# Two PSUM banks instead of three per leaf pair, the imaginary sum added by TensorE, and two block sums moved in the last batch

## The chip, the cores and the metric

The kernel runs on one core of a Trainium2 chip. The metric is the device time of one execution in microseconds; three runs are shown, and the profile comes from one further execution. The engines are named as in the profile: PE is TensorE (PEld its weight loads), DVE is VectorE, ACT is ScalarE, POOL is GpSimd, SP is SyncE, which here only issues DMAs.

## The reference

Two graph layers over 64 graphs of 256 nodes with 256 features each, all in float32. What matters here is the first layer's convolution branch:

```python
xc = jnp.transpose(x, (0, 2, 1))
h = relu(bn1(conv1d(xc, conv1_w)))            # kernel size 1
h = bn2(conv1d(h, conv2_w, pad=8))            # 17 taps, 256 -> 256 channels
x_conv = jnp.transpose(relu(h + xc), (0, 2, 1))
A = exp(-dist(x @ w_se.T)) * adj              # message passing
x_nmp = A @ relu(x @ w_msg.T + b_msg)
gi = concat([x_conv, x_nmp]) @ w_ih.T + b_ih  # a GRU cell: r, z and n parts
gh = x @ w_hh.T + b_hh
nn_ = tanh(gi_n + r * gh_n)
x1 = layernorm(x + (1 - z) * nn_ + z * x)
```

The second layer normalises x1, multiplies by the adjacency and by two weights, adds, applies relu, adds x1 and normalises again.

## The kernel before

The 64 graphs are worked in 8 batches of 8. Each batch has a convolution, `conv(b)`, which is a Python generator that emits a few instructions at a time, and each graph has a per-graph part (gates, message passing, update, second layer). While batch b's eight graphs are emitted, `pump()` (line 1180) takes steps from `conv(b + 1)` in between. The order of the instructions on every engine is the order of emission; nothing reorders it later[...]. The convolution of batch b+1 is therefore interleaved with the graphs of batch b at fixed places, the same in each of the batches 1 to 7. Batch 0's convolution runs alone at the start, and the graphs of batch 7 run alone at the end (lines 1246 to 1278).

The 17-tap convolution is done by transforms. DVE splits the signal by butterflies into leaves (`split_all`, `split_u`, lines 342 to 374); each leaf is a complex number per channel, held as a real slot `re` and an imaginary slot `im` in the SBUF tile XF, and `sums` slots hold re + im. A complex product takes three real products with the transformed weights: k1 = sums·w0, k2 = re·w1, k3 = im·w2, and then re' = k1 − k3 and im' = k1 + k2. Leaves are taken in pairs: `products(b, first, sums)` (line 389) emits the matmuls of one pair and returns a function `take` that is called later, after some butterflies, and brings the results to SBUF. There are seven such pairs per batch, numbered 0 to 6 below, and then `last_products` (line 429). Each real product gives 128 rows by 256 channels and is two matmuls of 128x256 (`product`, line 383), and every float32 matmul leaves two records in the trace, so a pair has 24 records.

The weights w0, w1, w2 of one leaf come by one DMA of 768 KB from DRAM into a buffer of a pool of three (`load_w`, line 376, `bufs=3`; the issue is line 380 on SP's queue). Loads take the three buffers in turn; a load's issue waits on SP's queue until the buffer's last reader, a matmul, is done, and everything behind it on SP waits too. In batch 0 the weights are all in SBUF already.

PSUM has eight banks, handed out in turn by `bank()` (line 100), so an allocation waits for the readers of the one eight before it.

For batch 0, `products` hands over to `products_added` (line 409), which has another form: it uses two banks, emits k1's matmuls (records 0 to 7 of the pair), has ACT copy k1 to SBUF (line 418), emits k3's (records 8 to 15), and then adds k2's matmuls onto the bank of k1 (records 16 to 23), so that TensorE forms im'. Its `take` copies im' with ACT (line 425) and forms re' with DVE (line 426). For batches 1 to 7 the three products go to three banks, leaf by leaf; `take` copies k1 with ACT (line 404) and forms re' and im' with DVE (lines 405 and 406).

In the last batch, `block_gates(k)` (line 814) forms the gates from block products, after `block_sums(k, i)` (line 798) has made sums of blocks of the operands on DVE, four operations for each of three operands (i = 0 for x, 1 for the passed messages, 2 for the convolution). Its fourth step is x's part of n: eight matmul records (line 856) and one DVE addition (line 858).

Of the kernel before, what the change touches and what calls it, by code (L numbers as in the profile page):

```python
# [17 lines left out]
B, N, D = 64, 256, 256  # L18
# [16 lines left out]
def leaf_angles(phi, m):  # L35

    if m == 1:
        return [phi]
    return leaf_angles(phi / 2, m // 2) + leaf_angles(phi / 2 + PI, m // 2)
# [8 lines left out]
LEAVES = [(V + k, V + 8 + k, a) for k, a in enumerate(leaf_angles(PI / 2, 8))]  # L48
# [28 lines left out]
def gnn_two_layers(  # L77
# [17 lines left out]
    nc = tc.nc  # L95
# [4 lines left out]
    def bank(name):  # L100
        return psum.tile([P, 512], F32, tag="ps", name=name)
# [143 lines left out]
    def sl(a, n, step=1):  # L245
        return X[:, a:a + n] if step == 1 else X[:, a:a + (n - 1) * step + 1:step]
# [129 lines left out]
    def load_w(b, first, n):  # L376
        if b == 0:
            return lambda m, c: W2[0][:, c, first + m, :]
        t = work.tile([P, 3, C, D], F32, tag="w2", name="w2", bufs=3)
        nc.sync.dma_start(out=t[:, :n], in_=w2m[first:first + n].rearrange("f c p o -> p f c o"))  # L380
        return lambda m, c: t[:, m, c, :]

    def product(ps, slot, w, m, first=True):

        for c in range(C):
            nc.tensor.matmul(ps, X[:, slot, c * P:(c + 1) * P], w(m, c), start=first and c == 0, stop=(c == C - 1),  # L386
                             skip_group_check=True)

    def products(b, first, sums):

        if b == 0:
            return products_added(first, sums)
        p1, p2, p3 = bank("ps_k1"), bank("ps_k2"), bank("ps_k3")
        re, im, _ = LEAVES[first]
        for k in range(2):
            w = load_w(b, 3 * (first + k), 3)
            at = slice(k * D, (k + 1) * D)
            product(p1[:, at], sums + k, w, 0)
            product(p2[:, at], re + k, w, 1)
            product(p3[:, at], im + k, w, 2)  # L400

        def take():
            k1 = sl(sums, 2).rearrange("p s e -> p (s e)")
            nc.scalar.copy(k1, p1)
            nc.vector.tensor_sub(sl(re, 2).rearrange("p s e -> p (s e)"), k1, p3)
            nc.vector.tensor_add(sl(im, 2).rearrange("p s e -> p (s e)"), k1, p2)
        return take

    def products_added(first, sums):

        p1, p3 = bank("ps_k1"), bank("ps_k3")
        re, im, _ = LEAVES[first]
        w = [load_w(0, 3 * (first + k), 3) for k in range(2)]
        at = [slice(k * D, (k + 1) * D) for k in range(2)]
        k1 = sl(sums, 2).rearrange("p s e -> p (s e)")
        for k in range(2):
            product(p1[:, at[k]], sums + k, w[k], 0, k == 0)
        nc.scalar.copy(k1, p1)
        for k in range(2):
            product(p3[:, at[k]], im + k, w[k], 2)  # L420
        for k in range(2):
            product(p1[:, at[k]], re + k, w[k], 1, False)

        def take():
            nc.scalar.copy(sl(im, 2).rearrange("p s e -> p (s e)"), p1)
            nc.vector.tensor_sub(sl(re, 2).rearrange("p s e -> p (s e)"), k1, p3)
        return take
# [222 lines left out]
    def load(k):  # L650

        if k >= B:
            return
        load_xt(k)
        load_adj(k)
# [9 lines left out]
    def load_x(k):  # L665
        if k < B:
            XG[k] = work.tile([P, C, D], F32, tag="x", name="x")
            nc.sync.dma_start(out=XG[k], in_=x[k].rearrange("(c p) d -> p c d", p=P))
# [129 lines left out]
    def block_sums(k, i):  # L798

        if i == 2:  # L800
            xc, g = XC[k]
            v = xc[:, :, g, :]
        else:
            v = (XT, NMP)[i][k]
        a11, a12, a21, a22 = (v[:, c, n * P:(n + 1) * P] for n in range(C) for c in range(C))
        at = S * D + ((k % 2) * 3 + i) * 4 * P
        s1, s2, s3, s4 = (XF[:, at + j * P:at + (j + 1) * P] for j in range(4))
        nc.vector.tensor_add(s1, a21, a22)
        nc.vector.tensor_sub(s2, s1, a11)
        nc.vector.tensor_sub(s3, a11, a21)  # L810
        nc.vector.tensor_sub(s4, a12, s2)
        LEFT[k, i] = (a11, a12, s4, a22, s1, s2, s3)
# [54 lines left out]
    def update(k):  # L867

        rz, gn = RZ[k]
        nn = work.tile([P, C, D], F32, tag="nn", name="nn", bufs=1)  # L870
        stt(nn, rz[:, :, :D], 1.0, gn[:, :, D:], op0=ALU.add, op1=ALU.mult)
        stt(nn, nn, 0.5, gn[:, :, :D])
        nc.scalar.activation(nn, nn, AF.Tanh)
        yield

        w = work.tile([P, C, D], F32, tag="w", name="w", bufs=1)
        nc.vector.tensor_sub(w, XG[k], nn)
        stt(w, rz[:, :, D:], 3.0, w, op0=ALU.add, op1=ALU.mult)
        stt(w, nn, 4.0, w)
        mv = work.tile([P, C, 2], F32, tag="mv", name="mv", bufs=4)  # L880
        for n in range(C):
            stats(mv, n, w[:, n, :])


        q = work.tile([P, 2, C], F32, tag="q", name="q", bufs=4)
        nc.gpsimd.tensor_scalar(q[:, 0, :], mv[:, :, 1], 4 * EPS, None, ALU.add)
        nc.gpsimd.tensor_scalar(q[:, 1, :], mv[:, :, 1], 1 + EPS, 4 * EPS * EPS, ALU.mult, ALU.add)
        nc.gpsimd.tensor_tensor(q, q, mhalf[:, :2 * C].rearrange("p (a c) -> p a c", a=2), ALU.pow)
        sh = work.tile([P, C], F32, tag="sh", name="sh", bufs=4)
        nc.gpsimd.tensor_mul(sh, mv[:, :, 0], q[:, 0, :])  # L890
        nc.gpsimd.tensor_scalar(sh, sh, -1.0, None, ALU.mult)  # L891
        yield
        H[k] = work.tile([P, C, D], F32, tag="h", name="h", bufs=1)
        X1[k] = work.tile([P, C, D], F32, tag="x1", name="x1", bufs=2)
        for n in range(C):
            nc.vector.tensor_scalar(H[k][:, n, :], w[:, n, :], mv[:, n, 0:1], q[:, 1, n:n + 1],
                                    ALU.subtract, ALU.mult)
        for n in range(C):
            nc.scalar.activation(X1[k][:, n, :], w[:, n, :], AF.Identity, bias=sh[:, n:n + 1], scale=q[:, 0, n:n + 1])  # L899
        yield  # L900


    def transposes_h(k):
        hT = work.tile([P, C, N], F32, tag="hT", name="hT", bufs=1)
        ps = bank("ps_hT")
        for c in range(C):
            for n in range(C):
                q = c * N + n * P
                nc.tensor.transpose(ps[:, q:q + P], H[k][:, n, c * P:(c + 1) * P], ident)
        for c in range(C):  # L910
            nc.scalar.activation(hT[:, c, :], ps[:, c * N:(c + 1) * N], AF.Identity,
                                 bias=gb[:, 1, c:c + 1], scale=gb[:, 0, c:c + 1])
        H[k] = hT

    def project(k):
        hT = H[k]
        hr = work.tile([P, C, D], F32, tag="hr", name="hr", bufs=1)
        outs = []
        for n in range(C):
            ps = bank("ps_out")  # L920
            for c in range(C):
                nc.tensor.matmul(ps, hT[:, c, n * P:(n + 1) * P], wrr[:, c, :], start=(c == 0), stop=(c == C - 1))  # L922
            nc.scalar.copy(hr[:, n, :], ps[:, :D])
            outs.append(ps)
        OUTS[k] = (hr, outs)
# [29 lines left out]
    def step(g):  # L955
        if g is not None:
            next(g, None)
# [103 lines left out]
    first = conv(0)  # L1061
# [114 lines left out]
    for b in range(NB):  # L1176
        coming = conv(b + 1) if b + 1 < NB else iter(())
        done, at, goal = 0.0, 0, BG * POINTS - 6
# [67 lines left out]
    for k in range(first_k, B - 1):  # L1246
        load(k + 3)
        load_x(k + 1)
        ga, up = block_gates(k), update(k)
        step(ga)  # L1250
        step(y_left)
        step(ga)
        transposes_h(k - 1)
        step(ga)
        passing(k + 1)
        if k + 2 < B:
            factors(k + 2)
        step(ga)
        if k + 2 < B:
            block_sums(k + 1, 0)  # L1260
            block_sums(k + 1, 2)
        project(k - 1)
        if k + 2 < B:
            distances(k + 2)
        msg = messages(k + 3) if k + 3 < B else None
        step(msg)
        step(up)
        step(msg)
        step(up)
        if k + 2 < B:  # L1270
            block_sums(k + 1, 1)
        step(up)
        if k + 2 < B:
            mask(k + 2)
        agg = aggregate(k - 1)
        step(agg)
        step(agg)
        y_left = agg
# [44 lines left out]
```

## Time and profile before

| | |
|---|---|
| median of three runs | 2246.47 us (2245.61 to 2249.44) |
| the profiled execution, its own time | 2248.85 us |
| its span (first to last instruction) | 2247.1 us |
| PE busy | 2205.1 us, 98% of the span |
| DVE busy | 1719.0 us, 76% |
| ACT busy | 773.1 us, 34% |
| POOL busy | 503.8 us, 22% |
| leaf products on PE, batches 1 to 7 (line 386) | 1316 records, 297.8 us |
| ACT copy of k1, batches 1 to 7 (line 404) | 49, 0.57 us each |
| DVE sum and difference from PSUM (lines 405, 406) | 49 each, 0.68 us each |
| load of one leaf's weights (line 380) | 105 of 768 KB, 5.8 us to landing in the median |

In the timeline a row is a stretch of equal instructions on one engine: start, length, engine, line, operation, tiles, form, count, and in brackets the engine's idle time ahead of it with what ended it. In the view of waits a row says who waited for whom: total us, times, the longest. A DMA row of SP or ACT is the issue, not the transfer.

### The profile page before, as it was taken

How to read it: one execution, taken by the hardware profiler on the slowest of the kernel's cores; microseconds unless marked ns; L12 is line 12 of the kernel's file. 1: busy time of each engine (PE TensorE's matmuls, PEld its weight loads, DVE VectorE, ACT ScalarE, POOL GpSimd, SP SyncE). 2: the span in 40 equal slices, each digit the busy share in tenths (PEclk: the TensorE clock that was granted, in tenths of full speed). 3: DMA queues.
4: the chain of work that ended last, by engine and by line, in shares of the span. 5: the costliest groups of instructions: out<-in, count | busy, mean ns of one | idle time of the engine just before them, and what ended most of it. 6: DMA issues, size and time to landing. Idle time of an engine off the chain costs nothing.

```text
span 2247.1 us, 24777 instructions
## 1 busy us (share of the span) xinstructions
PE 2205.1 (98%) x8400; PEld 1459.6 (65%) x8400; DVE 1719.0 (76%) x3322; ACT 773.1 (34%) x1594; POOL 503.8 (22%) x933
## 2 busy tenths in 40 slices
PE   8999999999999999999999999999999999999998
PEld 5776666666665676656666566666666666666665
DVE  6967988399873998649886598956989389896665
ACT  6533223532244322433224422243222532224333
POOL 0112222132122321223122231223222132122222
PEclk9999999999999999999999999999999999999999
DMA  5932442314323152233422243222432314421100
GB/s 149 318 113 66 141 135 77 103 38 151 121 76 108 54 169 83 75 103 108 139 87 76 84 131 122 76 96 69 141 116 90 99 42 137 141 71 43 43 28 20
DMA packets 212683, 226.70 MB, mean 101 GB/s; under 512 B 22103, under 2 KB 203854, under 8 KB 212558
## 3 DMA queue, kind: packets, MB, share of 16 engines
q1 hardware_dynamic: 190128, 191.27, 27.0%
q10 hardware_dynamic: 22430, 33.86, 4.3%
q8 instruction: 67, 1.10, 0.2%
q14 instruction: 58, 0.48, 0.1%
HBM read 179.22 MB, written 45.88 MB: 100 GB/s over the span
## 4 chain that ended last, share of the span: by engine, by line
PE 67%; DVE 24%; DMA 3%; issue 3%; POOL 2%; ACT 1%; SPq 0%; POOLq 0%; DVEq 0%; ACTq 0%
PE ps_k L386 14%; PE ps_rz L755 11%; DVE XF L104 9%; PE ps_rz L752 6%; PE ps_n L767 6%; PE ps_out L922 5%; PE ps_c L492 5%; PE ps_nmp L736 4%; DMA w<-w2m 3%; PE ps_msg L678 3%; PE ps_n L765 3%; PE ps_out L934 3%; DVE XF L362 2%; DVE XF L456 2%; DVE nn L104 1%
## 5 line engine op out<-in xcount | busy, mean ns | idle before, releaser
L104 DVE SCALAR_TENSOR_TENSOR XF<-XF 128x512 f32<-128x512 f32 (+2 forms) x800 | 508.0, 666 | 7.4
L386 PE MATMUL ps_k<-w,XF 128*128 128x256 f32 x1316 | 297.8, 381 | 17.6 <-DVE st L688 12.0
L386 PEld LDWEIGHTS ps_k<-w,XF 128*128 128x128 f32 x1316 | 246.7, 190 | 63.3 <-issue 24.9
L696 POOL TENSOR_TENSOR sq<-st 128x6 f32<-128x6 f32 x64 | 13.8, 215 | 1219.2 <-DVE st L688 1169.3
L922 PE MATMUL ps_out<-wrr,hT 128*128 128x512 f32 x504 | 226.7, 592 | 0.0
L759 ACT ACTIVATE rz<-rz 128x512 f32<-128x512 f32 x114 | 71.8, 630 | 446.4 <-DVE rz L758 446.4
L752 PE MATMUL ps_rz<-whh,xT 128*128 128x512 f32 x456 | 214.4, 592 | 0.0
L755 PE MATMUL ps_rz<-wih,nmp 128*128 128x512 f32 x456 | 214.3, 592 | 0.0
L755 PE MATMUL ps_rz<-wih,xc 128*128 128x512 f32 x456 | 214.3, 592 | 0.0
L768 DVE TENSOR_TENSOR gn<-ps_n,brzn 128x512 f32<-128x512 f32 x114 | 78.3, 687 | 171.2 <-PE ps_n L767 171.2
L899 ACT ACTIVATE x<-w,sh,q 128x256 f32<-128x256 f32 x126 | 68.8, 593 | 342.7 <-POOL sh L891 342.7
L755 PEld LDWEIGHTS ps_rz<-wih,xc 128*128 128x128 f32 x456 | 86.6, 190 | 109.1 <-issue 109.1
L755 PEld LDWEIGHTS ps_rz<-wih,nmp 128*128 128x128 f32 x456 | 86.6, 190 | 109.1 <-issue 109.1
L758 DVE TENSOR_TENSOR rz<-ps_rz,brzn 128x512 f32<-128x512 f32 x114 | 77.7, 682 | 104.3 <-PE ps_rz L755 104.3
L922 PEld LDWEIGHTS ps_out<-wrr,hT 128*128 128x128 f32 x504 | 95.2, 190 | 93.6 <-issue 81.8
L678 PE MATMUL ps_msg<-wms,xT 128*128 128x260 f32 x512 | 129.9, 396 | 0.0
L362 DVE TENSOR_TENSOR XF<-XF 128x512 f32<-128x512 f32 (+3 forms) x128 | 125.4, 1004 | 1.7
L736 PE MATMUL ps_nmp<-AT,msg 128*128 128x256 f32 x512 | 121.0, 379 | 0.0
L752 PEld LDWEIGHTS ps_rz<-whh,xT 128*128 128x128 f32 x456 | 82.1, 190 | 57.8 <-issue 55.0
L934 PE MATMUL ps_out<-hr,adj 128*128 128x256 f32 x504 | 119.5, 380 | 0.0
L492 PE MATMUL ps_c<-xTc,w 128*128 128x512 f32 x256 | 116.2, 596 | 2.3 <-ACT xTc L482 2.3
L765 PE MATMUL ps_n<-whh,xT 128*128 128x256 f32 x456 | 117.2, 379 | 0.0
(200 smaller groups left out, 3738.1 us busy)
## 6 DMA issues: line engine op xcount, KB each, us to landing
w<-w2m SPq DMA_DIRECT2D x105, 768.0 KB, 5.8
xn<-in_x_dram SPq DMA_DIRECT2D x32, 512.0 KB, 4.2
xt<-xTc ACTq DMA_DIRECT2D x32, 512.0 KB, 3.2
xT<-xt SPq DMA_DIRECT2D x64, 256.0 KB, 3.0
xb<-in_x_dram SPq DMA_DIRECT2D x32, 512.0 KB, 5.1
adj<-in_adjT_dram SPq DMA_DIRECT2D x64, 256.0 KB, 2.7
x<-in_x_dram SPq DMA_DIRECT2D x64, 256.0 KB, 3.0
out_dram<-y ACTq DMA_DIRECT2D x63, 256.0 KB, 2.3
```

The source lines that it names most:

```text
L104: nc.vector.scalar_tensor_tensor(o, in0, s, in1, op0=op0, op1=op1)
L362: (nc.vector.tensor_add if add else nc.vector.tensor_sub)(sl(o, n), sl(a, n), sl(b, n))
L386: nc.tensor.matmul(ps, X[:, slot, c * P:(c + 1) * P], w(m, c), start=first and c == 0, stop=(c == C - 1), skip_group_check=True)
L492: nc.tensor.matmul(pss[o], w1[:, c, o * P:(o + 1) * P], xTc[:, c, :], start=(c == 0), stop=(c == C - 1))
L678: nc.tensor.matmul(ps[:, :D + 4], XT[k][:, c, m * P:(m + 1) * P], wms[:, c, :], start=(c == 0), stop=(c == C - 1 and not idle))
L736: nc.tensor.matmul(ps[:, d * N:(d + 1) * N], MSG[k][:, m, d * P:(d + 1) * P], AT[k][:, m, :], start=(m == 0), stop=(m == C - 1))
L752: nc.tensor.matmul(prz, XT[k][:, c, q], whh[:, c, 0:2 * D], start=(c == 0), stop=False)
L755: nc.tensor.matmul(prz, ins[i], wih[:, i, 0:2 * D], start=False, stop=(j == 3))
L765: nc.tensor.matmul(pn[:, D:], XT[k][:, c, q], whh[:, c, 2 * D:], start=(c == 0), stop=(c == C - 1))
L767: nc.tensor.matmul(pn[:, :D], t, wih[:, i, 2 * D:], start=(i == 0), stop=(i == 3))
L922: nc.tensor.matmul(ps, hT[:, c, n * P:(n + 1) * P], wrr[:, c, :], start=(c == 0), stop=(c == C - 1))
L934: nc.tensor.matmul(po, ADJ[k][:, m, n * P:(n + 1) * P], hr[:, m, :], start=False, stop=(m == C - 1), skip_group_check=True)
```

## The change

`products` takes the form of `products_added` for every batch: two banks, k1 copied by ACT between the matmuls, k2 added onto k1's bank by TensorE, im' copied by ACT in `take`. Both leaves' weights are asked for at the start of the pair. In the last batch the block sums of x (0) and of the convolution (2) for the next graph are emitted ahead of the step of `block_gates` that adds x's part of n, instead of after it.

```diff
     def products(b, first, sums):

-        if b == 0:
-            return products_added(first, sums)
-        p1, p2, p3 = bank("ps_k1"), bank("ps_k2"), bank("ps_k3")
-        re, im, _ = LEAVES[first]
-        for k in range(2):
-            w = load_w(b, 3 * (first + k), 3)
-            at = slice(k * D, (k + 1) * D)
-            product(p1[:, at], sums + k, w, 0)
-            product(p2[:, at], re + k, w, 1)
-            product(p3[:, at], im + k, w, 2)
-
-        def take():
-            k1 = sl(sums, 2).rearrange("p s e -> p (s e)")
-            nc.scalar.copy(k1, p1)
-            nc.vector.tensor_sub(sl(re, 2).rearrange("p s e -> p (s e)"), k1, p3)
-            nc.vector.tensor_add(sl(im, 2).rearrange("p s e -> p (s e)"), k1, p2)
-        return take
-
-    def products_added(first, sums):
 
         p1, p3 = bank("ps_k1"), bank("ps_k3")
         re, im, _ = LEAVES[first]
-        w = [load_w(0, 3 * (first + k), 3) for k in range(2)]
+        w = [load_w(b, 3 * (first + k), 3) for k in range(2)]
         at = [slice(k * D, (k + 1) * D) for k in range(2)]
         k1 = sl(sums, 2).rearrange("p s e -> p (s e)")
         for k in range(2):
             product(p1[:, at[k]], sums + k, w[k], 0, k == 0)
         nc.scalar.copy(k1, p1)
         for k in range(2):
             product(p3[:, at[k]], im + k, w[k], 2)
         for k in range(2):
             product(p1[:, at[k]], re + k, w[k], 1, False)
 
         def take():
             nc.scalar.copy(sl(im, 2).rearrange("p s e -> p (s e)"), p1)
             nc.vector.tensor_sub(sl(re, 2).rearrange("p s e -> p (s e)"), k1, p3)
         return take
...
         passing(k + 1)
         if k + 2 < B:
             factors(k + 2)
-        step(ga)
-        if k + 2 < B:
             block_sums(k + 1, 0)
             block_sums(k + 1, 2)
+        step(ga)
         project(k - 1)
```

## The prediction

> **What bounds the kernel now.** I read the page first (busy time, chain), then the waits, then the timeline around the leaf products, engine by engine, and last the loads. The page's busy times and its chain:
>
> ```profile
> PE 2205.1 (98%) x8400; PEld 1459.6 (65%) x8400; DVE 1719.0 (76%) x3322; ACT 773.1 (34%) x1594; POOL 503.8 (22%) x933
> PE 67%; DVE 24%; DMA 3%; issue 3%; POOL 2%; ACT 1%; SPq 0%; POOLq 0%; DVEq 0%; ACTq 0%
> ```
>
> PE sets the time: it idles 42 us in all. So work taken from DVE gains nothing unless PE waits for it, and any new wait of PE is paid in full. The view of waits says what PE waits for at the leaf products and in the last batch:
>
> ```profile
> PE ps_k L386 <- DVE st L688: 12.0, 14, 0.9
> PE ps_k L386 <- DMA w<-w2m: 4.7, 12, 1.1
> PE ps_a L826 <- DVE XF L831: 7.7, 7, 1.8
> DVE XF L858 <- PE ps_n L856: 21.6, 7, 3.1
> ```
>
> The timeline of batch 2's first two pairs, from the rows of PE, ACT, POOL and SP:
>
> ```profile
> 516.88 10.60 PE L386 MATMUL ps_k<-w,XF 128*128 128x256 f32 x48 [0.38 <-DMA w<-w2m]
> 519.73 18.04 SPq L380 DMA_DIRECT2D w<-w2m  x5
> ...
> 520.98 2.25 POOL L946 TENSOR_TENSOR sh<-mv,q 128x2 f32<-128x2 f32 x1
> 523.32 2.27 POOL L947 TENSOR_SCALAR sh<-sh 128x2 f32<-128x2 f32 x1
> 525.62 1.09 ACT L950 ACTIVATE y<-y,sh,q 128x256 f32<-128x256 f32 x2 [4.51 <-POOL sh L947]
> 526.74 0.38 ACTq L951 DMA_DIRECT2D out_dram<-y  x1
> 527.16 0.59 ACT L404 COPY XF<-ps_k 128x512 f32<-128x512 f32 x1 [0.45 <-ACT y L950]
> ```
>
> Pairs 0 and 1 run without a break (48 records, 0.216 us apart). ACT is then held at L950, the second layer's normalisation of an earlier graph, which waits for POOL; the copy of k1 runs 10.28 us after the pair began, and today nobody minds. Pair 3 of the same batch, and batch 0, which has the new form already:
>
> ```profile
> 548.63 1.03 PE L386 MATMUL ps_k<-w,XF 128*128 128x256 f32 x4
> 550.58 4.55 PE L386 MATMUL ps_k<-w,XF 128*128 128x256 f32 x20 [0.92 <-DVE st L688]
> 550.86 0.63 ACT L692 ACTIVATE msg<-msg 128x512 f32<-128x512 f32 x1 [2.25 <-DVE msg L690]
> 551.40 0.57 ACT L404 COPY XF<-ps_k 128x512 f32<-128x512 f32 x1
> ```
>
> ```profile
> 81.15 21.12 PE L386 MATMUL ps_k<-w2all,XF 128*128 128x256 f32 x96
> 83.36 0.59 ACT L418 COPY XF<-ps_k 128x512 f32<-128x512 f32 x1 [1.70 <-PE ps_k L386]
> 86.77 0.59 ACT L425 COPY XF<-ps_k 128x512 f32<-128x512 f32 x1 [2.82 <-PE ps_k L386]
> ```
>
> In batch 0, ACT is idle and the copy (83.36 to 83.95) ends before PE comes to record 16 (81.15 + 16 x 0.216 = 84.6): no gap in 96 records.
>
> [...] So PE must hold k2's records until the copy has read the bank; batch 0 shows the order, not a wait. [...] L946, elsewhere 0.19 us at the least, takes 2.25 beside DVE's 128x2048 butterflies, which the change leaves in place. [...] The trace shows one such window, 7.50 to 10.90 us, at PEclk 0.50, after a window with PE busy 1.67 of 3.40; a later window with 1.62 of 3.40 busy was not followed by one.
>
> **The change, part by part.** Matmuls: the same 24 records per pair, no gain or loss in work. DVE loses 49 additions, 49 x 0.68 = 33 us; ACT gains 49 copies of 0.57, 28 us; both engines have room, neither sum reaches PE. What counts are the waits that move, per batch, times seven (the interleaving is the same in every batch).
>
> Pair 0. The copy of k1 now stands between the matmuls, but in ACT's order directly behind L951, where L404 stands today: it can start no sooner than now. PE comes to record 16 at 3.5 us after the pair's start (16 x 0.216) and waits until the copy's end, 0.59 + some 0.06 later. The seven starts of L404 less the seven starts of PE's stretch are 10.00, 10.28, 9.83, 10.28, 10.40, 10.22 and 10.34 us, 71.35 in all; less 7 x (3.5 - 0.65): **+51 us**, 7.3 each. L950 hangs on POOL and DVE work from before the pair, so it does not slip with PE. Behind the waiting PE stand the rest of pair 0, pair 1, the turning of h and the next gates; DVE and ACT wait for these in turn.
>
> Pair 1. It needs a buffer that pair 0's first leaf releases. Today that leaf's last reader is record 11 (issue 519.73), and the load is needed 24 records later at record 12 of pair 1: 5.0 us, against 4.7 to 5.1 to landing for this load, just in time (the 4.7 us of DMA waits above). In the new order the last reader is record 19, and the load is needed at record 4 of pair 1. With PE resuming at 0: issue at 1.05 (4 records, tail 0.17), landing at 5.9, need at 12 x 0.216 = 2.6. **+3.3 us**, x7 = +23. Behind it on SP stand the loads of pairs 2 and 3 and the next graph's x; they slip with PE, and those of pairs 2, 3, 5 and 6, 1.7 us later by the new order, keep some 3 us or more in hand.
>
> Pair 4. Its loads are issued three at once at 557.82 because SP hung on earlier buffers; the second lands 8.4 us after its issue at 558.34, at 566.7. Needed today at record 12 (567.3), then at record 4 (565.6): late by 1.0 to 1.7 in the seven batches. The copy behind L951 there (568.11 + 0.38, ends 569.1 against record 16 at 568.2) costs up to about the same and lies under it. **+1.3**, x7 = +9.
>
> Pairs 3 and 6. The bank that waits for DVE (0.86 us in the mean, 1.1 with its restart) is not among the two now used: their banks come from L726, long done. But the copy stands behind L692 (550.86) and the im' copy of the pair before (551.40): it starts at 551.9, ends 552.5, against record 16 at 548.63 + 3.45 = 552.1. Net **-0.7**, x14 = -10. Pairs 2 and 5: ACT is ready in time, 0. The butterflies that read im' now wait for ACT; its copy sits in L404's old place, ahead of them: 0.
>
> Clock. [...] I take half clock at the resume. Then the 4 records ahead of the load's issue last 0.8 us longer, and a part of the 3.4 us window left beyond the load's wait costs half of itself, about 0.7: **+1.5**, x7 = +10. From below 0 (no half clock); from above 3 per batch, 21.
>
> Last batch. DVE idles 3.1 us at L858 for PE in each graph; eight operations of 0.2 us start to start fit in that, 1.95 us in all. What comes free behind does not reach PE: after the block sums and two nn operations DVE waits 1.26 us at L688 for the messages' matmuls anyway, and L831, for which PE waits 1 us per graph, keeps its place. **0**. Without that cover it would cost 2 us x 6.
>
> Sum: 51 + 23 + 9 - 10 + 10 = **+83 us** on a span of 2247.1 gives 2330. The profiled execution took 2248.85, 2.4 over the median of 2246.47, which gives the same **2330 us**.
>
> **Rivals.** *Only the copy's wait*: the load of pair 1 arrives under the stall after all. For it: three buffers. Against: the releasing record lies behind the stall. 51 + 9 - 10 = +50, with the clock 2297 to 2307. *Deeper*: half clock lasts, or DVE, late with pair 0's `take` by about 1.2 us, holds PE later. Against: DVE then idles about 8 us for the gates. +100 to +120, 2347 to 2367. *Faster*: PE does not wait for L950, because the copy is served early as in batch 0; then the bank waits at pairs 3 and 6 (12 us) go, and 2235 remains. It decides where the copy starts within 1.0 us of record 7's end; today's place of L404 is some 8 us past that. *No effect*: gains and waits cancel, 2246; it would need stalls of under 2 us per batch.
>
> **How the numbers follow.** Both waits, with some clock loss: 0.80, 2312 to 2346 (without the clock 2320, less 1 us per batch for a faster load; with its upper bound 2341 and some spread). Copy alone 0.08, deeper 0.07, faster 0.04, no effect 0.01. About 0.2%, 4.5 us, can be told from no change. Range 2300 to 2350: it takes the likeliest one's bounds and part of both neighbours. Slower 0.95, same 0.01, faster 0.04.
>
> **What would show it.** PE rows of about 16 records, a gap of 7 us that ends on ACT, then 12 records, a gap of 1.5 to 3.3 that ends on the DMA, in each of seven batches; a wait "PE for ACT XF" of about 50 us; the 12 us for DVE L688 gone; PEclk at 0.5 for a window after each gap; the last 245 us as long as before. It would be wrong if ACT reached L950 earlier because POOL's two slow operations shrink, or if the loads of pair 1 landed in under 2 us.

## The result, and the profile after

| | before | after |
|---|---|---|
| median | 2247.95 us (2245.61 to 2251.47, 4 runs) | 2338.93 us (2337.74 to 2340.16, 4 runs) |
| ratio, with its 95% interval | | 1.0403 (1.0385 to 1.0421) |
| the profiled execution, its own time / span | 2248.85 / 2247.1 us | 2340.16 / 2338.3 us |

The kernel became 91 us slower; 2330 was predicted. One of the six runs of the experiment e7 below took 3308.15 us at a mean granted clock of 0.653 and is left out of e7's median, which would be 2241.88 us with it.

The page of the kernel after gives busy times, the shares of the chain that ended last, and the group of the leaf products (busy us, mean ns of one, then the idle time just before them and what ended most of it):

```profile
PE 2235.6 (96%) x8400; PEld 1475.3 (63%) x8400; DVE 1691.1 (72%) x3273; ACT 801.3 (34%) x1643; POOL 498.6 (21%) x933
PE 60%; DVE 26%; POOL 4%; DMA 4%; issue 3%; ACT 2%; ACTq 0%; SPq 0%; POOLq 0%; DVEq 0%
L386 PE MATMUL ps_k<-w,XF 128*128 128x256 f32 x1316 | 328.8, 405 | 78.1 <-ACT XF L399 42.1
```

PE carries out the same 8400 matmuls and is busy 30 us longer, all of it in line 386 (297.8 us before, 328.8 now, by a mean of 405 ns instead of 381): these ran at a lower clock in part (0.50), as the slices below show. The other 60 us are idle time. DVE lost 28 us of work and 49 instructions and the span grew all the same. The view of waits of the kernel after (who waits, for whom: total us, times, longest):

```profile
PE ps_k L386 <- ACT XF L399: 42.1, 16, 5.9
PE ps_k L386 <- DMA w<-w2m: 34.8, 28, 2.5
PEld ps_k L386 <- ACT XF L399: 52.9, 25, 6.3
DVE XF L839 <- PE ps_n L837: 10.4, 7, 2.9
```

The 12.0 us of PE for DVE's `st` are gone. In their place stand 42.1 us for ACT's copy of k1 (line 399; the third row is the same wait at the weight loads) and 34.8 us for weights, 4.7 us before. DVE waits 10.4 us for x's part of n instead of 21.6: the block sums fill that wait, as they were meant to, and nothing is gained by it (e2 below).

The timeline of batch 2 shows where the waits lie. The rows are those of PE and of ACT, from pair 0 to pair 4:

```profile
529.44 1.10 PE L386 MATMUL ps_k<-w,XF 128*128 128x256 f32 x4 [0.25 <-DMA w<-w2m]
532.44 2.86 PE L386 MATMUL ps_k<-w,XF 128*128 128x256 f32 x12 [1.90 <-DMA w<-w2m]
540.49 4.64 PE L386 MATMUL ps_k<-w,XF 128*128 128x256 f32 x12 [5.19 <-ACT XF L399]
547.39 6.27 PE L386 MATMUL ps_k<-w,XF 128*128 128x256 f32 x20 [2.26 <-DMA w<-w2m]
...
538.31 1.09 ACT L931 ACTIVATE y<-y,sh,q 128x256 f32<-128x256 f32 x2 [4.52 <-POOL sh L928]
539.43 0.38 ACTq L932 DMA_DIRECT2D out_dram<-y  x1
539.85 0.59 ACT L399 COPY XF<-ps_k 128x512 f32<-128x512 f32 x1 [0.45 <-ACT y L931]
...
574.82 3.62 PE L386 MATMUL ps_k<-w,XF 128*128 128x256 f32 x16
578.70 1.99 PE L386 MATMUL ps_k<-w,XF 128*128 128x256 f32 x8 [0.26 <-ACT XF L399]
591.78 2.86 PE L386 MATMUL ps_k<-w,XF 128*128 128x256 f32 x12 [0.76 <-DMA w<-w2m]
595.11 1.99 PE L386 MATMUL ps_k<-w,XF 128*128 128x256 f32 x8 [0.47 <-ACT XF L399]
```

Pair 0, which ran without a break, is now in three pieces. After four records PE waits 1.90 us for the second leaf's weights, which the new form needs eight records earlier. After sixteen it waits 5.19 us for the copy, and the copy stands behind line 931, which waits for POOL; the chain of ACT ends at 540.44, PE starts at 540.49. The next four records of pair 1 follow at once, and the twenty after them wait 2.26 us for a load. The twelve records behind the copy take 4.64 us, the twelve ahead of it 2.86: half clock (0.50) up to 544.1. The same stretch in slices of 3.4 us (length, then busy time and instructions of PE, PEld, DVE, ACT and POOL, then the granted clock, DMA share and GB/s):

```profile
533.90:537.30 3.40, 1.40 (x7) 0.89 (x5) 3.37 (x2) 0.00 (x0) 3.31 (x2) 1.00 0.00 1
537.30:540.70 3.40, 0.21 (x1) 0.21 (x2) 3.33 (x4) 1.68 (x3) 0.97 (x1) 0.50 0.10 35
540.70:544.10 3.40, 3.40 (x9) 2.68 (x10) 0.61 (x1) 0.00 (x0) 0.00 (x0) 0.50 0.25 50
544.10:547.50 3.40, 1.14 (x6) 0.69 (x4) 3.02 (x7) 0.59 (x1) 0.00 (x0) 0.99 0.89 286
547.50:550.90 3.40, 3.40 (x9) 2.69 (x10) 2.69 (x6) 0.59 (x1) 0.00 (x0) 0.51 0.48 169
...
2093.80:2097.20 3.40, 2.11 (x10) 1.34 (x10) 3.30 (x6) 2.94 (x8) 0.00 (x0) 1.00 0.00 0
2097.20:2100.60 3.40, 3.40 (x13) 2.94 (x13) 3.37 (x8) 0.68 (x2) 0.25 (x2) 0.50 0.47 154
```

Half clock (0.50) holds from 537.3 to 544.1, in the stall and behind it, and again (0.51 in the slice) from 547.5 to 550.9, behind the load's wait at 545 to 547. The last two rows are from the last batch, where one more slice at 0.50 follows an idle stretch of 1.29 us; the last section returns to them.

**The loss by place.** PE works through the same records of line 386 in both kernels, so the start of each in one run less its start in the kernel before is the delay up to there, and the growth of the delay over a stretch is what that stretch costs. The mean over the seven batches, in us per batch, for the kernel after and for the experiments that keep the form in all pairs (a minus sign is a gain):

| stretch | after | e3 | e5 | e6 | e8 |
|---|---|---|---|---|---|
| pair 0, records 0 to 4 (own second load) | 1.36 | 1.34 | 0.67 | 0.65 | 1.28 |
| pair 0, records 4 to 16 (copy) | 5.86 | 0.30 | 6.93 | 0.87 | 5.85 |
| pair 0, record 16 to pair 1 (clock) | 1.82 | 0 | 1.83 | 0.10 | 0.10 |
| pair 1, records 0 to 4 (load) | 2.47 | 3.43 | 0.33 | 0 | 3.42 |
| pair 1, record 4 to its end (clock) | 1.44 | 1.56 | -0.08 | -0.07 | 1.37 |
| pair 3, records 0 to 16 | -0.73 | -0.74 | -0.74 | -0.74 | -0.73 |
| pair 4, records 0 to 16 (load, copy) | 1.63 | 1.33 | 1.59 | 0.10 | 1.49 |
| pair 6, records 0 to 16 | -0.73 | -0.74 | -0.74 | -0.73 | -0.73 |

For the kernel after the column adds up to 13.1 us, 92 in seven batches. The last batch adds 1.2, and scattered small differences take about 2 off, which leaves the 91.2 by which the span grew.

### The profile page after: what moved, and what is told of

Read it like the earlier page. It is cut to its first block, busy times and chain, and to the rows that moved or that the text cites. A ratio compares the mean times of both kernels' runs of the same rounds, so it can differ in the third digit from the quotient of the medians.

```text
span 2338.3 us, 24741 instructions
## 1 busy us (share of the span) xinstructions
PE 2235.6 (96%) x8400; PEld 1475.3 (63%) x8400; DVE 1691.1 (72%) x3273; ACT 801.3 (34%) x1643; POOL 498.6 (21%) x933
## 4 chain that ended last, share of the span: by engine, by line
PE 60%; DVE 26%; POOL 4%; DMA 4%; issue 3%; ACT 2%; ACTq 0%; SPq 0%; POOLq 0%; DVEq 0%
PE ps_k L386 10%; PE ps_rz L736 10%; DVE XF L104 9%; PE ps_rz L733 5%; PE ps_n L748 5%; PE ps_out L903 5%; PE ps_c L473 4%; DMA w<-w2m 4%; PE ps_nmp L717 4%; PE ps_msg L659 3%; PE ps_n L746 2%; PE ps_out L915 2%; DVE bst L845 2%; DVE w L104 2%; DVE XF L437 2%
## 5 line engine op out<-in xcount | busy, mean ns | idle before, releaser
L386 PE MATMUL ps_k<-w,XF 128*128 128x256 f32 x1316 | 328.8, 405 | 78.1 <-ACT XF L399 42.1
L386 PEld LDWEIGHTS ps_k<-w,XF 128*128 128x128 f32 x1316 | 261.7, 203 | 139.4 <-ACT XF L399 52.9
```

## The experiments

Each kernel ran beside the kernel before on the same chip; the ratios and their 95% intervals are against its runs there, whose medians are 2247.4 to 2247.8 us.

### The two parts of the change by themselves

e1 is the kernel after with the block sums back in their old place; e2 is the kernel before with only the block sums moved, by the same lines the other way round. e1:

```diff
             factors(k + 2)
+        step(ga)
+        if k + 2 < B:
             block_sums(k + 1, 0)
             block_sums(k + 1, 2)
-        step(ga)
```

> The changed kernel with the block sums of the last batch put back behind the step of n. My theory: the whole loss comes from the leaf products of batches 1 to 7, so the time stays that of the changed kernel, 2339 us, within 2. Rival: the moved sums bring or cost something in the last batch (the changed trace is 1.2 us longer there); then 2337 to 2338, or, if they gained 2 us in each of six graphs, 2351.

Measured: 2340.99 us (2336.69 to 2343.92), ratio 1.0414 (1.0400 to 1.0429).

> The kernel before with the block sums moved alone. My theory: they fill idle time of VectorE and nothing that TensorE waits for moves, so 2247 us, within 0.1% of before. Rival: VectorE comes earlier to what TensorE waits for at L831 (1 us in each graph), up to 6 us faster; or the addition of n comes later, up to 12 us slower.

Measured: 2248.6 us (2245.95 to 2251.99), ratio 1.0004 (0.9996 to 1.0012). The form of the leaf products holds the whole loss; the block sums neither cost nor gain anything that can be measured. In e2's profile the last batch takes 1.2 us longer; the last section returns to it.

### The copy's place and the weights' buffers, each undone alone and both together

Two waits are disputed: for the copy behind ACT's line 931, and for the weights. e3 moves the convolution's steps ahead of the step of the second layer that holds ACT up; e4 is the same swap in the kernel before, as a control:

```diff
             gates_n(k, 0)
-            step(y_left)
             pump()
+            step(y_left)
```

e5 leaves the copy where it is and takes the weights apart: w0 and w2, which the new form reads first, come into one of four buffers, w1, which it reads last, into one of two of its own, by a DMA of its own that is issued after those of both leaves. Further lines, which are not shown, fit the last products and some tiles of the set-up and of the last batch to the new buffers. The first leaf's w0 and w2 are now free after record 11 and no longer after record 19, and a pair's leaves find four buffers instead of three:

```diff
-        cols += [c, d - c, c + d]
+        cols += [c, c + d, d - c]
...
-        t = work.tile([P, 3, C, D], F32, tag="w2", name="w2", bufs=3)
-        nc.sync.dma_start(out=t[:, :n], in_=w2m[first:first + n].rearrange("f c p o -> p f c o"))
-        return lambda m, c: t[:, m, c, :]
+        t = work.tile([P, 2, C, D], F32, tag="w02", name="w02", bufs=4)
...
+        nc.sync.dma_start(out=t, in_=w2m[first:first + 2].rearrange("f c p o -> p f c o"))
+        u = work.tile([P, C, D], F32, tag="w1", name="wone", bufs=2)
+        LATE.append(lambda: nc.sync.dma_start(out=u, in_=w2m[first + 2].rearrange("c p o -> p c o")))
+        return lambda m, c: u[:, c, :] if m == 1 else t[:, m // 2, c, :]
```

e6 has both edits.

> The changed kernel with the steps of the convolution that stand behind the normalisation of y (L950 before, L931 after) emitted ahead of it, so that pair 0's copy of k1 no longer stands behind ScalarE's wait for GpSimd; the copy itself, its count and the loads stay. My theory: pair 0's 7.2 us and the half clock go, the wait for pair 1's weights (some 3.3 us) and for pair 4's (1.4 us) stay, pairs 3 and 6 gain 1.5: 2248 + 7 x (3.3 + 1.4 - 1.5) = 2270 us. Rival 1, that the 49 further copies on ScalarE or the accumulation itself cost the time: then it stays near 2339. Rival 2, that half clock comes from the load waits too: 2270 + 7 x 2 = 2284.

> Control for the order: the kernel before with the same swap of the convolution's steps and the normalisation of y. My theory: in the old form nobody waits early for that copy, so 2247 us, within 0.2%. If the swap itself moves the time, the other run is to be read against this one.

> The changed kernel with a leaf's weights in two buffers: w0 and w2, read ahead of the wait for the copy, in one of four, w1, read behind it, in one of two; as many bytes, two loads per leaf instead of one. The order on all engines but SP stays. My theory: pair 1's first weights come ahead of pair 0's wait, so pair 1's load wait (2.5 us and the part of the clock behind it) and pair 4's (1.4 us) go; pair 0's 7.2 us and its half clock (1.8 us up to pair 1, perhaps 1.5 in pair 1) stay, and the copy of pair 4 keeps about 1 us: 2248 + 7 x (7.2 + 1.8 + 1.0 + 1.0 - 1.5) = 2315 us. Rival, that the load wait lies under the clock's recovery or that further issues cost SP: 2339 or more.

> Both: the convolution's steps ahead of the normalisation of y, and the weights in two buffers. My theory: all of pair 0's, pair 1's and pair 4's waits go and the gain of pairs 3 and 6 (0.73 us each, 14 times) is left: 2248 - 10 = 2238 us, 0.4 to 0.5% under before. Rival: something else of the new form costs (the copies, the accumulation): 2248 or more.

Measured:

| | weights in three buffers | weights in split buffers |
|---|---|---|
| copy behind line 931 | after: 2338.93, ratio 1.0403 (1.0385 to 1.0421) | e5: 2315.1, 1.0294 (1.0280 to 1.0307) |
| copy ahead of it | e3: 2301.29, 1.0238 (1.0224 to 1.0252) | e6: 2246.93, 0.9995 (0.9987 to 1.0003) |

The control e4 took 2246.4 us, ratio 0.9998 (0.9990 to 1.0007): the swap by itself does nothing.

Both waits are real, and together they are the whole loss: without both, the kernel takes the time of the one before. The 49 further copies and the accumulation, which the rivals of e3 and e6 name, are all there in e6; the table leaves no loss for them but the 1.5 us per batch at pair 0, which is traced below. The two waits aren't independent: undone singly they give back 37.6 and 23.8 us, 61 in all, and together 92. The timeline of e3 shows why. PE in batch 2, pairs 0 and 1:

```profile
522.56 1.10 PE L386 MATMUL ps_k<-w,XF 128*128 128x256 f32 x4 [0.39 <-DMA w<-w2m]
524.79 5.45 PE L386 MATMUL ps_k<-w,XF 128*128 128x256 f32 x24 [1.13 <-DMA w<-w2m]
533.53 7.48 PE L386 MATMUL ps_k<-w,XF 128*128 128x256 f32 x20 [3.29 <-DMA w<-w2m]
```

The copy's stall is gone (records 4 to 28 run in one piece), but the load for pair 1 is now late by 3.29 us instead of 2.26, and the twenty records behind it take 7.48 us, against 6.27 in the kernel after and 4.58 at full clock (e8 below). The slices of e3 at that place:

```profile
532.60:536.00 3.40, 2.47 (x6) 2.00 (x7) 3.33 (x6) 0.36 (x1) 0.00 (x0) 0.50 0.74 242
536.00:539.40 3.40, 3.40 (x10) 2.64 (x9) 3.23 (x8) 1.21 (x3) 0.00 (x0) 0.50 0.25 82
```

So in e3 half clock (0.50 in both slices) stands behind a load's wait with no stall ahead of it, as e3's second rival said. The expectation of 2270 was 31 us too low, and the rival's 2284 still 17. Two things make 20 of them, 7 x (1.34 + 1.56): it left out that pair 0's own second load is late by 1.34 us in each batch (in the kernel after it had lain ahead of the stall, whose end the copy sets, so that it seemed to cost nothing), and it gave the load's wait no clock loss of its own (1.56). A rest of the copy's wait (0.30 per batch) and the loss in the last batch are 3 more, and the profiled execution, to which these numbers belong, was 3 us below the median; the remainder is spread over small differences.

e5 confirms the other half. Its PE rows in batch 2, pairs 0 and 1 (the line numbers are 11 higher in this kernel, and `wone` is w1):

```profile
528.52 2.86 PE L397 MATMUL ps_k<-w,XF 128*128 128x256 f32 x12 [1.17 <-DMA w<-w2m]
537.78 3.78 PE L397 MATMUL ps_k<-wone,XF 128*128 128x256 f32 x8 [6.40 <-ACT XF L411]
541.35 4.03 PE L397 MATMUL ps_k<-w,XF 128*128 128x256 f32 x16
545.21 1.89 PE L397 MATMUL ps_k<-wone,XF 128*128 128x256 f32 x8
```

The wait for the copy is 6.40 us instead of 5.19: PE comes to record 16 earlier, mostly because the load ahead of it is less late (by 0.69 us in the mean), and the copy doesn't come earlier with it. Pair 1 has next to no wait left (0.33 us in the mean), and no loss behind it (-0.08). Its two rows in the table fall from 2.47 and 1.44 us to nearly nothing, which with the 0.69 less at pair 0's load and the 1.07 more at the copy makes 23 of the 23.8 us between the two medians. That 2315 was met to the microsecond is partly luck: the clock loss that was expected in pair 1 (1.0 us per batch) did not come (-0.08), while pair 0's stall cost 0.4 more than put down, pair 4 cost 0.6 more, and 0.33 of the load's wait stayed.

e6 was expected at 2238 and missed by 9 us; its rival said 2248 or more. The timeline of e6, batch 2, pair 0 (PE and ACT):

```profile
517.80 2.86 PE L397 MATMUL ps_k<-w,XF 128*128 128x256 f32 x12 [0.99 <-DMA w<-w2m]
521.06 1.99 PE L397 MATMUL ps_k<-wone,XF 128*128 128x256 f32 x8 [0.40 <-ACT XF L411]
...
519.91 0.63 ACT L753 ACTIVATE rz<-rz 128x512 f32<-128x512 f32 x1 [2.92 <-DVE rz L752]
520.44 0.57 ACT L411 COPY XF<-ps_k 128x512 f32<-128x512 f32 x1
```

The copy, moved ahead of line 931's wait, stands behind the next one: the tanh of r and z (line 753), which waits for DVE. It starts at 520.44, and PE waits 0.40 us here; the stretch costs 0.87 in the mean over the batches. With 0.65 us for the load this makes 1.5 us per batch, which takes all of the 1.47 that pairs 3 and 6 gain.

### The clock, taken away by itself

e8 asks what the stall's half clock costs. It is the kernel after, with twelve matmuls of 128x256 added between k3's and k2's records in pair 0 of the batches 1 to 7; this is work added, into a bank that nobody reads, so that PE isn't idle in the stall:

```diff
             product(p3[:, at[k]], im + k, w[k], 2)
+        if b > 0 and first == 0:
+            fill = bank("ps_fill")
+            for _ in range(12):
+                nc.tensor.matmul(fill[:, :D], X[:, im, :P], w[0](2, 0), start=True, stop=True)
```

> The changed kernel with 12 further matmuls of 128x256 (24 records, 5.2 us) into a bank that nobody reads, in pair 0 of batches 1 to 7, between the records of k3 and those of k2: TensorE works through the wait for the copy instead of idling; nothing else is changed and no work is left out. My theory: the wait is set by ScalarE's queue and stays as long, but [...] the half clock behind it goes: 1.8 us in pair 0 and about 0.5 in pair 1, in seven batches: 2339 - 16 = 2323 us. If the slow records behind the gap had another cause (weights arriving, the bank), or if the load wait of pair 1 brings half clock by itself as in the third run, 2339 to 2330. If the fill itself were on the path, 2375.

Measured: 2333.48 us (2330.3 to 2338.24), ratio 1.0383 (1.0366 to 1.0400): 5.5 us less than the kernel after, within the rival's 2339 to 2330 and not at 2323. The slowest of these runs reaches the range of the kernel after (from 2337.74), so the rows and the table carry this experiment more than its total. PE in batch 2 of e8:

```profile
534.48 5.34 PE L405 MATMUL ps_fill<-w,XF 128*128 128x256 f32 x24
540.30 2.86 PE L386 MATMUL ps_k<-w,XF 128*128 128x256 f32 x12 [0.48 <-ACT XF L399]
546.44 4.58 PE L386 MATMUL ps_k<-w,XF 128*128 128x256 f32 x20 [3.27 <-DMA w<-w2m]
```

PE resumes after the same wait as in the kernel after (5.85 and 5.86 us per batch in the table), and the twelve records behind the copy take 2.86 us instead of 4.64. But 0.95 us per batch of the 1.72 saved there are given back at once: PE comes to the load 1.72 us sooner, and the load, whose issue waits for record 19 alone, lands only about 0.8 sooner (6.0 to 6.1 us after the start of record 16, where its landing shows, instead of 6.8 to 6.9), so its wait grows from 2.47 to 3.42. This settles two terms. The load of pair 1 by itself is late by 3.4 us (e3 says the same, 3.43). And the loss behind that load (1.37) goes with the load's wait and not with the stall, behind which next to nothing is lost here (0.10). It is a mean over the batches: in the one shown, the twenty records take 4.58 us and the granted clock is 1.00 in every slice from 533.90 to 550.90.

So the stall's own half clock is worth 1.72 less 0.95, about 0.8 us per batch, once the wait behind it is counted: 7 x 0.77 = 5.4 in all, close to the 5.5 between the medians.

### Keeping the form where it gains

Pairs 3 and 6 gained 0.73 us each in every run of the table. e7 is the kernel before with the new form in pairs 2, 3, 5 and 6 (first leaves 4, 6, 10 and 12); e9 has it in pairs 3 and 6 alone, which this diff shows:

```diff
-        if b == 0:
-            return products_added(first, sums)
+        if b == 0 or first in ADDED:
+            return products_added(b, first, sums)
...
+    ADDED = (6, 12)
```

> The kernel before, with the new form of the products only in pairs 2, 3, 5 and 6 of batches 1 to 7 and the old one, three banks, in pairs 0, 1 and 4; the block sums as before. My theory: no wait at pairs 0, 1 and 4, and the gain at pairs 3 and 6 if the banks that fall to them are again early ones: 2238 us. Rival: with other banks in turn (the old pairs take three), pairs 3 and 6 meet VectorE's bank again: 2248; or the copy stands in the way: above.

> The kernel before with the new form in pairs 3 and 6 alone. My theory: pairs 2 and 5 gave nothing by themselves, so as in the seventh run 2242 us, 0.2 to 0.4% under before, if pairs 3 and 6 still meet an early bank. Rival: with three banks in pairs 2 and 5 the turn of the banks is another and VectorE's bank is met again: 2247.

Measured: e7 2239.85 us (2236.33 to 2244.12), ratio 0.9960 (0.9945 to 0.9974); e9 2238.39 us (2236.15 to 2241.93), ratio 0.9959 (0.9947 to 0.9972). Both are faster than the kernel before by 0.4%, 8 us for e7 and 9 for e9; the new form in pairs 2 and 5 adds nothing to it that can be measured. The timeline of e9, pair 3 of batch 2 (PE and ACT):

```profile
548.99 5.87 PE L386 MATMUL ps_k<-w,XF 128*128 128x256 f32 x24
551.22 0.63 ACT L694 ACTIVATE msg<-msg 128x512 f32<-128x512 f32 x1 [2.25 <-DVE msg L692]
551.76 0.57 ACT L406 COPY XF<-ps_k 128x512 f32<-128x512 f32 x1
552.22 0.59 ACT L420 COPY XF<-ps_k 128x512 f32<-128x512 f32 x1
```

Here k1's copy (line 420) ends at 552.81, and record 16 comes at 548.99 + 3.45 = 552.44: the wait is under 0.4 us. The bank that used to wait for DVE is not asked for, so the break of about a microsecond after four records, which the kernel before has there, is gone.

## Why the prediction was right, and where it was not

**The mechanism** held at every place that was named: a stall that ends on ACT after record 16 of pair 0, then twelve records, then a wait for the DMA, in all seven batches; DVE's relief, which reaches nothing; the wait for DVE's `st`, which disappears. The wait for the copy itself came out at 42.1 us, not about 50; a part of the difference PE had spent ahead of it in each batch, waiting for pair 0's second load (1.36 us in the mean). Of the rivals, "only the copy's wait" is refuted by e5, which takes the load's lateness away and gains 24 us; "faster" by the stall itself; "no effect" by the result. "Deeper" lies at 2347 and above, and 2338.93 was measured; its first half, that half clock lasts, came true in part (10.2 us at 0.50 in six of the seven batches and 6.8 in one, where the sum reckoned with a part of 3.4), and its second, that DVE holds PE later, shows nowhere: behind pair 1 the table has no loss but pair 4's, which is the load's and the copy's. By term, in us for all seven batches:

| term | predicted | measured |
|---|---|---|
| pair 0, to record 16 | +51 | 7 x (1.36 + 5.86) = 50.5 |
| pair 1, its load | +23 | 17.3 as it stands; 24 where no half clock precedes it (e3, e8) |
| clock, both places | +10 | 12.7 + 10.1 = 22.8 |
| pair 4 | +9 | 11.5 |
| pairs 3 and 6 | -10 | -10.2 |
| last batch | 0 | +1.2 |
| small differences elsewhere | not named | -2 |

**Pair 0** came out to 0.5 us, because the reason held on which the sum rested: the end of the copy is set by POOL and DVE, not by PE, so the wait could be read from the starts that the profile before shows. That PE holds k2's records until the copy has read the bank was an assumption, since no trace of the kernel before shows such a wait; in batch 2 of the kernel after PE starts at 540.49, 0.05 us behind the copy's end. The cause of the loss was told too simply. Of the 7.2 us, 1.36 are the pair's own second load, needed eight records earlier than before, which the prediction named for pair 4 and not for pair 0. In the sum it makes no difference, since the end of the copy sets the end of both. It did matter as soon as the copy was moved: e3's expectation fell on it.

**The clock** is the term that was mis-sized, and it is most of what is missing between 83 and 91. That half clock stands at the resume was an estimate of the author's; the trace after has it in all seven batches (0.50 for 6.8 us, from 537.31 to 544.14 in batch 2). The first part of the term, 0.8 us per batch for the slow records ahead of the load's issue, was right: e8 gives 0.8. The step that failed is the second, "a part of the 3.4 us window left beyond the load's wait costs half of itself, about 0.7": 1.44 us were measured there, and not from a rest of the half clock at the stall. In six of the seven batches the clock is back at 1.00 for 3.4 us, and then at 0.50 for another 3.4 us, behind the load's wait; e3 and e8 lose 1.56 and 1.37 us there without the stall's half clock. The sum had no term for this, though the signs to look for speak of half clock after each gap. The load's own reckoning held: the prediction had its issue 1.05 us after PE resumes and its landing at 5.9, and in e3, with no half clock ahead, they come 1.06 and 5.9 to 6.2 us after record 16's start. Pair 1's load and the clock belong together, because the slower records ahead of the load shorten its wait: together they cost 12.7 + 17.3 + 10.1 = 40 us against the 23 + 10 predicted. That is 7 of the 8 us, 5 of them by the second part of the clock (7 x 0.74).

**Pair 4** was predicted from its load, with the copy under it. In e5, where the load is on time (0.09 us in records 0 to 4), the copy alone costs 1.50; in e3, where the copy is out of the way, the load alone costs 1.33. So either one costs about as much as the two together (1.63), as was said, and the size was 0.3 per batch too small.

**The last batch** was right in its argument: in e5, which also has the block sums moved, it ends 0.03 us earlier than before. The 1.2 us in the kernel after go with a slice at half clock (2097.20 to 2100.60, 0.50); e1, with the block sums in their old place, is longer there too, so they are not the block sums'. The prediction of an equal last stretch is therefore wrong by that number and not by its reasoning.

## What to carry to other kernels

In this kernel a read-back of a PSUM bank between two accumulations put TensorE behind everything that was queued on the reading engine at that place (42.1 us of waits for the copy), so the cost is read from that engine's row in the timeline before the change: from the start of the copy that stands there today, less the time at which TensorE would come to it. An order that reads all of one operand first and another last also moves the need for the next weights forward and the release of the last ones back, and a pool of three buffers that was just in time is then late by the sum of both (here eight records and eight, 16 x 0.216 = 3.5 us; 3.4 were measured). Where each wait hides part of another, take the form at the places where it gains (here two pairs of seven, 9 us) instead of repairing it everywhere (e6, nothing gained).

## What the runs showed of the hardware

**Where half clock stood.** The mean granted clock of the profiled executions was 0.984 in the kernel after, 0.988 in e5 (the load's wait nearly gone), 0.993 in e3 (the stall gone), 0.994 in e8 (the stall filled), and 0.999 in e6, which has little left of either wait; the kernel before has 0.998. In the kernel after six of the seven batches have 6.8 us at 0.50 at the stall and 3.4 us behind the load's wait, and one, batch 4, has the 6.8 us alone. PE was not idle throughout ahead of them: in the slices shown with the result it was busy for 1.40 and for 1.14 us of the 3.40 ahead. In batch 2 of e8 PE waits 3.27 us for the same load and no half clock follows (1.00 in every slice from 533.90 to 550.90). Why one wait has it behind it and another hasn't was not shown.

**A wait inside a stretch at half clock.** In e3's two slices above PE is busy for 2.47 us of 3.40 in the first, which holds the end of the load's wait, and both are at 0.50; the next slice, from 539.40, is at 1.00. That is how twenty records came to take 7.48 us.

**The last batch.** Ahead of the distances PE idles for 1.30 us in the kernel before (line 724) and for 1.29 in the kernel after (line 705), and is busy for 2.10 and 2.11 us of the 3.40 that hold the wait. After (the last two slices shown with the result) the next slice is at 0.50. Before it is not:

```profile
2002.00:2005.40 3.40, 2.10 (x7) 0.61 (x5) 3.40 (x7) 1.91 (x5) 0.00 (x0) 1.00 0.00 0
2005.40:2008.80 3.40, 3.40 (x21) 2.79 (x22) 3.26 (x5) 1.53 (x5) 0.00 (x0) 1.00 0.39 108
```

What makes the difference was not shown. The last stretch is 1.1 to 1.6 us longer in the kernel after, e1, e2, e3, e6, e7 and e8 than in the kernel before, and not in e4, e5 and e9. A difference of a microsecond between two versions of this kernel is for that reason no evidence on an edit made in the last batch: e2's 1.2 us are not the block sums', since e5 has the sums moved and loses nothing there, and e1 loses it without the sums moved.

**A slower clock can be free.** Here half clock in front of a wait for a load cost only what the wait didn't take back: filling the stall in e8 saved 7 x 1.72 = 12 us of slow records, and 7 x 0.95 = 6.7 of it went into the longer wait.
